# Attention over 8192 context keys: the transposition of a quarter of the softmax integers, and the spreading of the key scales, by other engines

## The chip, the cores and the metric

The kernel runs on one core of one Trainium2 chip. The core has a matrix engine (PE, whose weight loads are listed apart as PEld), a vector engine (DVE), a scalar engine (ACT), a GpSimd engine (POOL) and a sync engine (SP), which mainly issues transfers. ACT and POOL issue transfers too; sixteen DMA engines carry them all. Each engine works through its own instructions in order and waits on semaphores for the others.

The metric is the device time of one execution in microseconds (us), lower is better. Before the change the median of three runs is 2955.57 us (2953.47 to 2957.51).

## The reference, cut to what matters

The program is one block of a perceiver: cross attention of 512 queries on 8192 context tokens, then causal self attention inside each of four sequences, then a feed-forward layer with 4-bit weights. The change touches only the cross attention (and the place of one small load):

```python
q = ((layernorm(x) @ Wq + bq) * scale)        # 512 queries, 16 heads of 64
k, v = split(ctx @ Wkv + bkv)                 # 8192 keys and values
q = _fq_sym(q, axis=-1)                       # integers -127..127 times a scale, per query and head
k = _fq_sym(k, axis=-1)                       # the same, one scale per key and head
v = _fq_sym(v, axis=2)                        # one scale per column of v, over all keys
attn = softmax(einsum('bhqd,bhkd->bhqk', q, k))
attn = _fq_unsigned(attn, axis=-1)            # integers 0..255, scale = row maximum / 255
out = einsum('bhqk,bhkd->bhqd', attn, v) @ Wp + bp
```

So for each head and each query there are 8192 scores. They are products of integers, multiplied by the scale of the key, exponentiated with the row maximum taken off, rounded to integers of 0 to 255, and multiplied with the integers of v. The integers are kept as 16-bit numbers.

## The kernel before

**Stages.** Queries are projected first. Then two passes over the context project the values (V pass) and the keys (K pass), each matrix product in three parts; PE is the engine that is always busy there. In the K pass the keys are quantised on DVE, transposed by a transfer from on-chip memory to on-chip memory (`transpose_k`, L564, a `dma_start_transpose` on SP's queue, 128x512 of 16 bits at a time), copied to a staging tile by ACT (`store_k`, L568) and written to device memory `k_d` by POOL's queue. `key_scales` (L589) does the same for the scales of a quarter of the keys: PE transposes, ACT copies, POOL writes to `sk_d`. The order of the work of these stages is written out by hand: `do(step, function, arguments)` puts an entry on an agenda, and `perform` runs it sorted by step.

**The attention stage** (L711 to L867) then works through 64 units, a unit being one head `h` of 16 and one tile `t` of 128 queries out of 4. A unit has eight groups `g` of 1024 keys. A loop over steps `s`, one group of scores per step, calls the following functions in a fixed order, each with its own lag:

- `scores` (L728), at step `s` for unit `s // 8`: two PE products into PSUM (tile `sc`, two buffers), then one DVE instruction (L748) that multiplies them by the scales of the keys (tile `sk`), writes them as `e`, and keeps the maximum.
- `maximum` (L759), after the eighth group: two small DVE instructions that make the row offset `m`.
- `exponentials` (L771), at groups 0 and 4 of the next unit: one ACT instruction (L776) over 4096 keys, `e` to 16-bit integers `a` (three buffers).
- `transposes` (L785), `LAG_T` = 12 steps behind the scores: four PE transposes of two keys at a time, since they treat pairs of 16-bit integers as one 32-bit word, into PSUM tile `a_pt` (three buffers); then one copy to on-chip memory, tile `aT`. The copy is on DVE for groups 0 and 4 (`COPIES_DVE`), on ACT for the other six.
- `values` (L799), `LAG_V` = 15 steps behind: eight PE products of `aT` with the values `vq`, summed up in PSUM tile `av`. After the last unit of a head four more DVE instructions finish the head (`r`, `xo`).

The tiles that a head needs are loaded during the last query tile of the head before: the keys `kt` (`load_keys`, four of 256 KB) and the scales `sk` (`load_scales`, eight transfers that write 1024 scales to each of 128 partitions, 512 KB each), both on SP's queue. The values of two heads at a time are loaded by `load_values` (L718) as four transfers of 512 KB on POOL's queue, into one of two buffers of 64 groups. Apart from those, SP and POOL have nothing to do in this stage.

**Other lines the change touches.** `shifts` (L369/L370) is a table of 1 KB, loaded on SP's queue ahead of everything else and used in the V pass. L678 is the place of the last `key_scales` in the agenda, at 5 behind the end of the K pass; `store_k` of the last tile stands at 4.

Of the kernel before, what the change touches and what calls it, by code (L numbers as in the profile page):

```python
# [32 lines left out]
F32 = mybir.dt.float32  # L34
BF16 = mybir.dt.bfloat16
# [10 lines left out]
P = 128  # L46
# [15 lines left out]
LAG_V = NSC + 7  # L62
COPIES_DVE = (0, 4)
# [20 lines left out]
def tile_perceiver(  # L84
# [132 lines left out]
    def do(step, fn, *args):  # L217
        agenda.append((step, len(agenda), fn, args))
# [151 lines left out]
    nc.sync.dma_start(out=shifts, in_=nibbles)  # L370
# [77 lines left out]
    do(0.5, load_bq)  # L448
    do(0.5, nc.vector.memset, vmax, 0.0)
# [117 lines left out]

    def store_k(u, n):  # L568
        if u % 2 == 0:
            ksts[n] = pools["k"].tile([P, NP // 2, 256], BF16, name="kst", tag=f"kst{n}", bufs=1)  # L570
        kst = ksts[n]
        nc.scalar.copy(  # L572
            kst.rearrange("p h (n e) -> p h n e", e=2)[:, :, :, u % 2], kTs.pop((u, n))
        )
        if u % 2 == 1:
            c, at_tile = divmod(u, KC // P)
            group, block = divmod(at_tile // 2, SC // 256)
            half, at_block = divmod(block, SC // 512)
            at_key = 512 * group + 256 * at_block
            hs = H // 2 * n  # L580
            for j in range(2):
                nc.gpsimd.dma_start(
                    out=k_d[c][
                        hs + j : hs + H // 2 : 2, half, :, at_key : at_key + 256
                    ].rearrange("p d n -> d p n"),
                    in_=kst[D * j : D * j + D],
                )

    def key_scales(c):  # L589

        row = pools["k"].tile([P, P, 2], F32, name="sk_row", tag="sk_row", bufs=1)
        for e in range(2):
            pt = kv_ps.tile([P, P], F32, name="sk_pt", tag="ps")
            nc.tensor.transpose(pt, sks[c].rearrange("p h (i e) -> p e h i", e=2)[:, e], ident)
            nc.scalar.copy(row[:, :, e], pt)
        nc.gpsimd.dma_start(
            out=sk_d[c].rearrange("h (i n) -> (h i) n", n=2 * P), in_=row.rearrange("p n e -> p (n e)")
        )
# [8 lines left out]
    def load_keys(h, c):  # L607
        kt = pools["keys"].tile([P, KC // 2], BF16, name=f"kt{h}_{c}", tag="kt", bufs=5)
        nc.sync.dma_start(out=kt, in_=k_d[c][h].rearrange("f d n -> (f d) n"))
        kts[h, c] = kt  # L610

    def load_scales(h, g):
        t = pools["keys"].tile([P, SC], F32, name=f"sk{h}_{g}", tag="sk", bufs=9)
        c, half = divmod(g, 2)
        nc.sync.dma_start(out=t, in_=sk_d[c][h, ts(half, SC)].partition_broadcast(P))
        sks_at[h, g] = t
# [45 lines left out]
    for u in range(KT):  # L662
# [14 lines left out]
        if u % (KC // P) == KC // P - 1:  # L677
            do(at + TILE + (5 if u + 1 == KT else 9.5), key_scales, u // (KC // P))  # L678
# [32 lines left out]
    with tc.tile_pool(name="at", bufs=2) as at, tc.tile_pool(  # L711
        name="at_s", bufs=4
    ) as small, tc.tile_pool(name="sc_ps", bufs=2, space=PSUM) as sc_ps, tc.tile_pool(
# [4 lines left out]
        def load_values(p):  # L718
            vq = at.tile([P, KT, P], F16, name=f"vq{p}", tag="vq")
            for c in range(NKC):  # L720
                part = ts(c, KT // NKC)
                nc.gpsimd.dma_start(out=vq[:, part, :], in_=vq_d[p, :, part, :])
            vqs[p] = vq
# [61 lines left out]
        def transposes(n, g):  # L785
# [9 lines left out]
            copy = nc.vector.tensor_copy if g in COPIES_DVE else nc.scalar.copy  # L795
            copy(aT, pt.bitcast(I32))  # L796
            state[n]["aT", g] = aT

        def values(n, g):  # L799
# [4 lines left out]
            aT = state[n].pop(("aT", g)).bitcast(F16).rearrange("p i (q e) -> p i e q", e=2)  # L804
            for i in range(SC // P):
                k = g * (SC // P) + i
                nc.tensor.matmul(  # L807
                    avs[h][:, t, :],
                    lhsT=aT[:, i // 2, i % 2, :],
                    rhs=vqs[p][:, k, ts(j, D)],  # L810
                    start=(k == 0),
                    stop=(k == KT - 1),
                )
            if g < NSC - 1:
                return
# [22 lines left out]
        load_values(0)  # L838
# [8 lines left out]
        with tc.manual_schedule():  # L847
            for s in range(n_steps + LAG_V):
                n, g = divmod(s, NSC)
                if g % (NSC // NEC) == 0 and 1 <= n <= len(units):  # L850
                    exponentials(n - 1, g // (NSC // NEC))
                if n < len(units):
                    h, t = units[n]
                    scores(n, g)
                    if t == NT - 1 and h + 1 < H:
                        if g % 2 == 1:
                            load_keys(h + 1, g // 2)
                        load_scales(h + 1, g)
                    if g == NSC - 1:
                        maximum(n)  # L860
                if at_step(s - LAG_T):
                    transposes(*at_step(s - LAG_T))
                if at_step(s - LAG_V):
                    values(*at_step(s - LAG_V))
                pair, at_pair = divmod(s, 8 * NSC)
                if at_pair == LAG_V and pair + 1 < NP:
                    load_values(pair + 1)  # L867
# [558 lines left out]
```

## Time and profile before

The profiled execution took 2952.94 us, 2.6 us under the median of the three runs; its span, from the first to the last instruction, is 2951.2 us. Of the engines in the whole span and in one unit of the attention stage (10.80 us from one unit's first scores to the next's, away from a change of head):

| engine | busy in the span, us | share | busy in one unit of 10.80 us |
|---|---|---|---|
| PE | 2766.8 | 94% | 8.7 to 9.5 |
| DVE | 2485.6 | 84% | 10.73 |
| ACT | 1342.0 | 45% | 10.58 |
| POOL | 270.5 | 9% | 0 |
| DMA engines, mean | | 44% | 1% to 66% |

The span's rows of tenths cut it into 40 equal slices of 73.8 us. The attention stage lies in slices 20 to 29: its first scores are multiplied on DVE at 1513.24 us, its last at 2218.30 us, and the last product of the values is done at 2233.6 us. An instruction's line can be that of a helper; tile names come without their buffer numbers.

### The profile page before, as it was taken

The numbers are of one execution on the slowest core, as the hardware profiler recorded it, in microseconds if no ns is written. First come the engines' busy times: TensorE is split into PE (matmuls) and PEld (weight loads), VectorE is DVE, ScalarE is ACT, GpSimd is POOL, SyncE is SP. The second block draws the span as 40 slices with busy tenths as digits, with TensorE's granted clock in tenths as the row PEclk, the third lists the DMA queues.
The fourth block names the chain that finished last, engine by engine and source line by source line (L and its number), as shares of the span: only waits on it lengthen the run. The fifth ranks groups of instructions, "written<-read, shape, count | busy, mean of one in ns | idle before, by whom it ended". The sixth has DMA issues, their size and how long they took to land.

```text
span 2951.2 us, 43061 instructions
## 1 busy us (share of the span) xinstructions
PE 2766.8 (94%) x16504; PEld 2166.9 (73%) x16504; DVE 2485.6 (84%) x4074; ACT 1342.0 (45%) x1537; POOL 270.5 (9%) x416
## 2 busy tenths in 40 slices
PE   8999999999999999999978888888888899799998
PEld 3788888888878888888846666666665677688876
DVE  6899998555799998988779999999995898776674
ACT  4212112112323333333249999999995244333332
POOL 0011111000022222222110000000001000000000
PEclk9999999999999999999989999999999999899999
DMA  5555565222457777776354424424413222122222
GB/s 182 176 201 195 192 219 188 93 100 93 145 143 195 189 193 187 196 182 167 90 187 149 161 108 165 172 108 150 159 62 119 68 84 67 50 86 98 95 86 93
DMA packets 203470, 412.76 MB, mean 140 GB/s; under 512 B 91904, under 2 KB 95616, under 8 KB 203264
## 3 DMA queue, kind: packets, MB, share of 16 engines
q1 hardware_dynamic: 158688, 256.37, 27.8%
q0 software_dynamic: 43520, 152.60, 16.2%
q8 instruction: 129, 2.11, 0.3%
q10 hardware_dynamic: 1056, 1.05, 0.2%
q14 instruction: 77, 0.63, 0.1%
HBM read 286.72 MB, written 104.34 MB: 133 GB/s over the span
## 4 chain that ended last, share of the span: by engine, by line
PE 67%; DVE 26%; issue 4%; DMA 2%; ACT 1%; SPq 0%; POOL 0%; DVEq 0%; ACTq 0%
PE kv_a L341 31%; DVE e L748 16%; PE kv_b L341 15%; PE acc_a L984 3%; PE y_a L1329 3%; PE gate_a L162 3%; PE up_a L162 3%; DVE aT L796 2%; PE q_ps L290 2%; PE y_b L1329 1%; PE acc_b L984 1%; PE gate_b L162 1%; PE up_b L162 1%; DVE sw_l L155 1%; PE a_pt L791 1%
## 5 line engine op out<-in xcount | busy, mean ns | idle before, releaser
L341 PE MATMUL kv_b<-w_d,c_d 128*128 128x512 f32 x2048 | 806.0, 394 | 0.8 <-DVE c_d L156 0.8
L341 PE MATMUL kv_a<-w_h,c_h 128*128 128x512 f32 x2048 | 806.4, 394 | 0.0
L341 PE MATMUL kv_a<-w_l,c_l 128*128 128x512 f32 x2048 | 806.1, 394 | 0.2 <-ACT w_l L244 0.2
L748 DVE CUSTOM_DVE_ANT_0 e<-sc,sk 128x1024 f32<-128x1024 f32 x512 | 600.7, 1218 | 9.9 <-DMA k_d<-kst 8.6
L776 ACT ACTIVATE a<-e,m,sq 128x4096 int16<-128x4096 f32 x128 | 487.6, 3809 | 29.7 <-DVE m L765 29.7
L341 PEld LDWEIGHTS kv_a<-w_l,c_l 128*128 128x128 f32 x2048 | 384.8, 188 | 89.8 <-ACT w_l L244 0.6
L341 PEld LDWEIGHTS kv_b<-w_d,c_d 128*128 128x128 f32 x2048 | 384.8, 188 | 89.8 <-DVE c_d L156 1.1
L341 PEld LDWEIGHTS kv_a<-w_h,c_h 128*128 128x128 f32 x2048 | 384.9, 188 | 88.9 <-issue 0.2
L791 PE MATMUL a_pt<-ident,a 128*128 128x128 f32 x2048 | 338.4, 288 | 6.8 <-ACT aT L796 3.7
L152 ACT ACTIVATE c_h<-c_raw 128x1024 fp32r<-128x1024 f32 x128 | 135.0, 1055 | 420.1 <-PE kv_a L341 413.0
L355 DVE SCALAR_TENSOR_TENSOR f<-kv_a,bkv 128x512 f32<-128x512 f32 x256 | 175.9, 687 | 163.9 <-PE kv_a L341 163.2
L791 PEld LDWEIGHTS a_pt<-ident,a 128*128 128x128 f32 x2048 | 216.4, 142 | 127.1 <-issue 64.5
L741 PE MATMUL sc<-kt,qT 64*128 64x512 bf16 x1024 | 203.4, 390 | 97.1 <-DVE mx L748 93.2
L572 ACT CAST kst<-kT 128x512 bf16<-128x512 int16 x128 | 99.4, 777 | 309.3 <-DMA kT<-ki 309.2
L807 PE MATMUL av<-vq,aT 128*128 128x64 f16 x4096 | 203.3, 193 | 11.4 <-DVE xo L822 11.4
L807 PEld LDWEIGHTS <-aT 128*128 128x128 f16 x4096 | 189.8, 98 | 19.9 <-issue 14.0
L796 ACT COPY aT<-a_pt 128x512 int32<-128x512 int32 x384 | 198.8, 593 | 1.3 <-PE a_pt L791 1.1
L356 DVE SCALAR_TENSOR_TENSOR f<-kv_b,f 128x512 f32<-128x512 f32 x256 | 176.7, 690 | 20.0 <-DVE f L355 1.4
L155 DVE TENSOR_TENSOR fw_l<-fw_raw,fw_h 128x1024 fp32r<-128x1024 f32 x64 | 78.3, 1224 | 107.1 <-ACT fw_h L152 106.9
L155 DVE TENSOR_TENSOR c_l<-c_raw,c_h 128x1024 fp32r<-128x1024 f32 x128 | 155.8, 1217 | 6.6 <-ACT c_h L152 6.2
L741 PEld LDWEIGHTS <-qT 64*128 64x128 bf16 x1024 | 67.3, 93 | 125.7 <-issue 96.2
L156 DVE SCALAR_TENSOR_TENSOR c_d<-c_l,c_raw 128x1024 fp32r<-128x1024 f32 x128 | 156.3, 1221 | 2.3
(186 smaller groups left out, 3763.5 us busy)
## 6 DMA issues: line engine op xcount, KB each, us to landing
c_raw<-in_ctxT SPq DMA_DIRECT2D x128, 512.0 KB, 3.6
sk<-sk_d SPq DMA_DIRECT2D x128, 512.0 KB, 6.7
v_d<-f POOLq DMA_DIRECT2D x64, 512.0 KB, 3.1
vl<-v_d POOLq DMA_DIRECT2D x64, 512.0 KB, 4.2
gu_d<-w_ffn POOLq DMA_DIRECT2D x44, 512.0 KB, 3.1
fw_raw<-gu_d SPq DMA_DIRECT2D x42, 512.0 KB, 3.3
k_d<-kst POOLq DMA_DIRECT2D x128, 128.0 KB, 3.6
vq_d<-vq POOLq DMA_DIRECT2D x32, 512.0 KB, 5.2
```

The costliest lines, as they stand in the source:

```text
L155: nc.vector.tensor_tensor(lo, src, hi, ALU.subtract)
L156: nc.vector.scalar_tensor_tensor(df, lo, -1.0 - UP, src, ALU.mult, ALU.add)
L162: nc.tensor.matmul(ps, lhsT=lhs(i, k), rhs=rhs(i, k), start=(k == 0 and i != 1), stop=(k == NC - 1 and i != 0),)
L341: nc.tensor.matmul(ps, lhsT=tokens[s][i][:, k, :], rhs=w3[s < KT][k][i][:, ts(n, 512)], start=(k == 0 and i != 1), stop=(k == NC - 1 and i ...
L355: nc.vector.scalar_tensor_tensor(f, a, 1.0 + 1.0 / UP, bias[s < KT][n], ALU.mult, ALU.add)
L356: nc.vector.scalar_tensor_tensor(f, b, -1.0 / UP, f, ALU.mult, ALU.add)
L741: nc.tensor.matmul(ps[:, ts(i, 512)], lhsT=qT[rows, h, ts(t, P)], rhs=kts[h, g // 2][rows, ts(g % 2, 512)], start=True, stop=True,)
L748: nc.vector.tensor_tensor_reduce(out=state[n]["e"][-1][:, ts(g % (NSC // NEC), SC)], in0=ps, in1=sks_at[h, g], scale=1.0, scalar=LOWEST, o ...
L776: nc.scalar.activation(a, st["e"][c], AF.Exp, bias=st["m"], scale=sq[:, t, h : h + 1], accum_out=sums[h][:, t, c : c + 1],)
L791: nc.tensor.transpose(pt[:, i, :], a[:, at_word + P * i : at_word + P * i + P], ident)
L796: copy(aT, pt.bitcast(I32))
L807: nc.tensor.matmul(avs[h][:, t, :], lhsT=aT[:, i // 2, i % 2, :], rhs=vqs[p][:, k, ts(j, D)], start=(k == 0), stop=(k == KT - 1),)
```

## The change

It does five things.

1. **A quarter of the keys (`DMA_KC` = 1, groups 2 and 3 of each unit) is no longer transposed by PE.** `dma_transposes` issues one transposing transfer per unit on SP's queue, 128x2048 integers of `a` into a tile `aT_d` (two buffers). It is called at step 4 of the next unit; the products of these two groups come 20 steps behind their scores (`LAG_D`), those of the other groups 16 instead of 15.
2. **Only group 4 is copied by DVE** (`COPY_DVE`); groups 0, 1, 5, 6 and 7 by ACT.
3. **The scales of a head are spread by POOL.** `load_rows` brings the scales of a head as four rows of 8 KB to partitions 0, 32, 64 and 96; `spread_scales` is a GpSimd `partition_broadcast` of 1024 of them to 128 partitions, eight for a head, in place of the eight transfers of 512 KB. The first head's scales still come by transfer. The scales get 8 buffers instead of 9, the keys 6 instead of 5, and the keys are asked for at groups 0 to 3 instead of 1, 3, 5 and 7.
4. **The values come in quarters** with five buffers of 16 groups (`order` puts the quarter of the transferred keys last), each asked for as soon as its buffer is read out.
5. **Small moves:** `shifts` is loaded at agenda step 32; the last `key_scales` goes from 5 to 3.9, ahead of `store_k` of the last tile; the keys of the transferred quarter are stored in plain order instead of even and odd ones interleaved (`in_order`), since the transfer keeps single integers apart and PE's transposition pairs; the small pool `at_s` is opened ahead of `at`.

```diff
-LAG_V = NSC + 7
-COPIES_DVE = (0, 4)
+LAG_V = NSC + 8
+COPY_DVE = 4
+DMA_KC = 1
+LAG_D = NSC + 12
...
-    nc.sync.dma_start(out=shifts, in_=nibbles)
...
+    do(32, lambda: nc.sync.dma_start(out=shifts, in_=nibbles))
...
+    def in_order(t, c):
+        dims = "p h" if len(t.shape) == 3 else "p"
+        if c == DMA_KC:
+            return t.rearrange(f"{dims} (e n) -> {dims} n e", e=2)
+        return t.rearrange(f"{dims} (n e) -> {dims} n e", e=2)
...
-        nc.scalar.copy(
-            kst.rearrange("p h (n e) -> p h n e", e=2)[:, :, :, u % 2], kTs.pop((u, n))
-        )
+        nc.scalar.copy(in_order(kst, c)[:, :, :, u % 2], kTs.pop((u, n)))
...
-        kt = pools["keys"].tile([P, KC // 2], BF16, name=f"kt{h}_{c}", tag="kt", bufs=5)
+        kt = pools["keys"].tile([P, KC // 2], BF16, name=f"kt{h}_{c}", tag="kt", bufs=6)
...
+    def tile_of_scales(h, g):
+        sks_at[h, g] = pools["keys"].tile([P, SC], F32, name=f"sk{h}_{g}", tag="sk", bufs=NSC)
+        return sks_at[h, g]
...
-            do(at + TILE + (5 if u + 1 == KT else 9.5), key_scales, u // (KC // P))
+            do(at + TILE + (3.9 if u + 1 == KT else 9.5), key_scales, u // (KC // P))
...
-        def load_values(p):
-            vq = at.tile([P, KT, P], F16, name=f"vq{p}", tag="vq")
+        def load_values(p, c):
+            vqs[p, c] = at.tile([P, KT // NKC, P], F16, name=f"vq{p}_{c}", tag="vq", bufs=NKC + 1)
+            nc.gpsimd.dma_start(out=vqs[p, c], in_=vq_d[p, :, ts(c, KT // NKC), :])
+
+        def load_rows(h):
+            sks_at[h] = at.tile([P, KC], F32, name=f"sk_row{h}", tag="sk_row", bufs=1)
             for c in range(NKC):
-                part = ts(c, KT // NKC)
-                nc.gpsimd.dma_start(out=vq[:, part, :], in_=vq_d[p, :, part, :])
-            vqs[p] = vq
+                nc.gpsimd.dma_start(out=sks_at[h][32 * c : 32 * c + 1, :], in_=sk_d[c][h : h + 1, :])
+
+        def spread_scales(h, g):
+            c, half = divmod(g, 2)
+            nc.gpsimd.partition_broadcast(
+                tile_of_scales(h, g), sks_at[h][32 * c : 32 * c + 1, ts(half, SC)], channels=P
+            )
...
-            copy = nc.vector.tensor_copy if g in COPIES_DVE else nc.scalar.copy
+            copy = nc.vector.tensor_copy if g == COPY_DVE else nc.scalar.copy
...
+        def dma_transposes(n):
+            at_key = DMA_KC * KC % EC
+            a = state[n]["a"][DMA_KC * KC // EC][:, at_key : at_key + KC].bitcast(F16)
+            aT = at.tile([P, KC // P, P], F16, name="aT_d", tag="aT_d")
+            nc.sync.dma_start_transpose(out=aT, in_=a)
...
-        load_values(0)
+        order = [c for c in range(NKC) if c != DMA_KC] + [DMA_KC]
+        load_rows(1)
...
-            for s in range(n_steps + LAG_V):
+            for s in range(n_steps + LAG_D):
                 n, g = divmod(s, NSC)
+                if s == 1:
+                    for c in order:
+                        load_values(0, c)
+                if g == NSC // NEC and 1 <= n <= len(units):
+                    dma_transposes(n - 1)
                 if g % (NSC // NEC) == 0 and 1 <= n <= len(units):
                     exponentials(n - 1, g // (NSC // NEC))
...
                     if t == NT - 1 and h + 1 < H:
-                        if g % 2 == 1:
-                            load_keys(h + 1, g // 2)
-                        load_scales(h + 1, g)
+                        if g < NKC:
+                            load_keys(h + 1, g)
+                        spread_scales(h + 1, g)
+                        if g == NSC - 1 and h + 2 < H:
+                            load_rows(h + 2)
...
-                if at_step(s - LAG_T):
-                    transposes(*at_step(s - LAG_T))
-                if at_step(s - LAG_V):
-                    values(*at_step(s - LAG_V))
-                pair, at_pair = divmod(s, 8 * NSC)
-                if at_pair == LAG_V and pair + 1 < NP:
-                    load_values(pair + 1)
+                for lag, work, dma in (
+                    (LAG_T, transposes, False),
+                    (LAG_V, values, False),
+                    (LAG_D, values, True),
+                ):
+                    at_lag = at_step(s - lag)
+                    if at_lag and (at_lag[1] * SC // KC == DMA_KC) == dma:
+                        work(*at_lag)
+
+                pair, since = divmod(s - NSC * (2 * NT - 1), NSC * 2 * NT)
+                if 0 <= pair < NP - 1 and since in (0, LAG_V + 1, LAG_V + 5, LAG_V + 7):
+                    load_values(pair + 1, order[(0, LAG_V + 1, LAG_V + 5, LAG_V + 7).index(since)])
```

## The prediction

> **What bounds the kernel now.** I read the share of busy time first, then the waits of the attention stage, then one unit of it in order of time. The page's rows of tenths show where each engine is full:
>
> ```profile
> PE   8999999999999999999978888888888899799998
> ...
> DVE  6899998555799998988779999999995898776674
> ACT  4212112112323333333249999999995244333332
> ```
>
> PE is full outside the attention stage; inside it (slices 20 to 29) DVE and ACT both are. Which of the two ends last? The waits between 1520 and 2220 us (who waited, for whom: total, times, longest):
>
> ```profile
> PE sc L741 <- DVE mx L748: 84.6, 191, 1.0
> ...
> ACT a L776 <- DVE m L765: 29.5, 62, 1.3
> ```
>
> PE and ACT wait for DVE, ACT once in each unit, and no wait of DVE's is anywhere near: between 1700 and 1900 us DVE's multiply L748 has 0.0 us of idle time before it. So DVE sets the pace. Its instructions in one unit (start, duration, us):
>
> ```profile
> 1600.46 1.23 DVE L748 CUSTOM_DVE_ANT_0 e<-sc,sk 128x1024 f32<-128x1024 f32 x1
> ...
> 1601.61 0.69 DVE L796 COPY aT<-a_pt 128x512 int32<-128x512 int32 x1
> 1602.21 1.22 DVE L748 CUSTOM_DVE_ANT_0 e<-sc,sk 128x1024 f32<-128x1024 f32 x1
> ...
> 1603.35 1.22 DVE L748 CUSTOM_DVE_ANT_0 e<-sc,sk 128x1024 f32<-128x1024 f32 x1
> ...
> 1611.13 0.21 DVE L765 TENSOR_SCALAR m<-m,nsq 128x1 f32<-128x1 f32 x1
> 1611.26 1.22 DVE L748 CUSTOM_DVE_ANT_0 e<-sc,sk 128x1024 f32<-128x1024 f32 x1
> ```
>
> Instructions overlap by some 0.08 us, so count from start to start: a multiply takes 1.145 (1602.21 to 1603.35), a copy behind it adds 1602.21 - 1600.46 - 1.145 = 0.605, and from the last multiply's end to the next unit's first 0.44 go to `m`. A unit is 8 x 1.145 + 2 x 0.605 + 0.44 = 10.81; measured 10.80.
>
> **Part 1, one copy less on DVE.** A unit becomes 9.16 + 0.605 + 0.44 = 10.20. The copy of group 0 of each unit runs inside the next one, so it leaves DVE's path 63 times (the 64th is in the drain): 63 x 0.605 = **-38.1 us**, if nothing else is late.
>
> *ACT, next in line.* From the same timeline: an exponential starts at 1600.56, its three copies at 1604.36, the next exponential at 1605.79, so 3.80 and 0.48 per copy in sequence: 10.46 per unit with six. With five it is 9.98, under 10.20 by 0.2. That thin margin is what is late next.
>
> *PE* does eight of its 32 transposes less. A step holds scores 0.32, transposes 0.49, values 0.33 (starts at 1604.63, 1604.98, 1605.47, 1605.80): 1.14 at most before. With the new lags, steps 0, 1, 4, 5 hold all three, steps 2, 3 no values, steps 6, 7 two groups of values (0.98). It stays under DVE's 1.145 everywhere and gains slack. The PSUM buffers: six groups rotate over three, each copied by ACT or DVE before its turn, as now.
>
> **Part 2, the transposing transfer.** The nearest row is the K pass's transfer of a quarter of the size (SP's issue min/median/max ns, and time to landing):
>
> ```profile
> L566 SPq DMA_TRANSPOSE kT<-ki x128: 1189/1191/2864, 808.5 to 1504.7; - x128
> ...
> DMA to landing us min/median/max: 2.4/3.1/9.2
> ```
>
> Issue: four times 1.19 = 4.8 us of SP's queue, if it goes with size. Bytes: the first of them, alone on the engines, shows as
>
> ```profile
> 809.50:810.00 0.50, 0.50 (x4) 0.41 (x3) 0.50 (x1) 0.00 (x0) 0.00 (x0) 1.00 0.55 111
> 810.00:810.50 0.50, 0.50 (x3) 0.39 (x3) 0.50 (x2) 0.00 (x0) 0.09 (x1) 1.00 0.76 152
> ```
>
> (last two columns: DMA share, GB/s): 0.5 x 111 + 0.5 x 152 = 131 KB for 0.655 us of all sixteen engines, 200 GB/s. So 512 KB need 2.6 us. [...] Landing is then about 4.8 + 1.7 = 6.5 us after the start (from the median 3.1 - 1.19 = 1.9 behind the issue); bounds: 3.1 (issue doesn't grow) and 4 x 3.1 = 12.4. The exponential ends 3.9 us into a unit, and PE wants the result at step 6 of the unit after, about 16.5: a cover of 12.6 us. The second cover is shorter: tile `a` has three buffers, and ACT's second exponential of the next unit overwrites it at 15.4, 11.5 us after the start. At 6.5 us both hold; at 12.4 ACT would lose 0.9 per unit. Cost taken: 0. On SP's queue behind it are only the keys of the next head, and it is behind theirs for one unit in four: the fourth key load waits for group 3's scores, at about 5.2 instead of 3.9, and 1.3 of 11.5 us is spent.
>
> DMA load falls: eight broadcasts of 512 KB per head go, four transposing transfers of 512 KB come.
>
> **Part 3, spreading by GpSimd.** A spread may start when the multiply of the same group has read the buffer, and must be done for that group a unit later. If a spread takes T, the eighth ends 1.15 + 8T into the head's last unit, and is wanted at 10.20 + 7 x 1.145 + 0.605 = 18.8: **T up to 2.2 us costs nothing**. No spread is in the trace. Its bounds by POOL's own rows (us, mean ns):
>
> ```profile
> L522 POOL PARTITION_ALL_REDUCE vall<-vmax x1 | 3.2, 3247 | 12.8 <-DVE ki L187 12.8
> ...
> masks.py:199 POOL TENSOR_SCALAR_AFFINE_SELECT ident<-ident 128x128 f32<-128x128 f32 x1 | 0.3, 293 | 0.3 <-POOL ident masks.py:197 0.3
> ...
> masks.py:197 POOL MEMSET ident<- 128x128 f32 x1 | 0.2, 204 | 0.3 <-POOLq L1416 0.3
> ```
>
> A memset of one column takes 101 ns, so writing costs (204 - 101) / 128 = 0.8 ns an element: 0.9 us for 1024, the low end. The all-reduce on 128x1024 reduces over partitions and then spreads: 3.25, the high end. Reading one operand and writing it, the select, comes to (293 - 101) / 128 = 1.5 ns, **1.6 us**; it is the nearest and I take it. [...] By 1.6 the eighth is done at 13.9, 4.9 us early; by 2.2 the sum is the same, with no cover left.
>
> Does a busy POOL slow DVE? The later adds on POOL show both cases:
>
> ```profile
> 2343.17 5.82 POOL L934 TENSOR_TENSOR x<-x,row 128x512 f32<-128x512 f32 x4 [87.84 <-DMA row<-in_abo]
> 2343.56 0.69 DVE L996 SCALAR_TENSOR_TENSOR f<-acc_b,f 128x512 f32<-128x512 f32 x1
> ...
> 2346.22 1.65 DVE L1052 TENSOR_TENSOR f<-f,cs 128x512 f32<-128x512 f32 x1
> ```
>
> With both operands in on-chip memory (L1052) DVE takes 1.65 instead of its median 0.69; with one operand in PSUM (L996) it takes its usual 0.69. The multiply reads `sc` from PSUM, the copy reads PSUM alone: cost 0. Only the `xo` product might meet a spread.
>
> POOL's queue: the row loads and value quarters are issues of 0.53 us each. A quarter is asked for when PE has read the buffer and is needed 7 steps (8.9 us) later at the tightest; four loads at once landed in 6.0 at the median. Nothing waits. Keys: six buffers, asked for earlier; nothing.
>
> **Part 4, the ends.** `shifts` off SP's queue lets the first load of x start at 0.73 instead of 1.18: -0.4 (ends 0 and -0.5), the chain starts with it; at its new place SP is idle. With `key_scales` ahead, its store no longer stands between the last casts and the last key stores on POOL (0.56 us): the stage starts 0.4 earlier, as the first multiply waits for those stores. Pipeline fill: the values come later by the four row loads (2.1 us), to about 1521, wanted at 1533. Drain: after the last exponential ACT does five copies instead of six: -0.5; the last transposing transfer lands before. The plain order of stored keys changes only an access pattern of ACT, which idles there.
>
> **Sum:** 38.1 + 0.4 + 0.4 + 0.5 = 39.4. Profiled: 2952.9 - 39.4 = 2913.5; the median of the runs lies 2.6 above the profiled one, so **2916 us**.
>
> **Rivals.**
> - *The spread is the bound (slower).* At T = 3.25 the eighth spread ends at 27.1, DVE stalls 8.3 us at each of 15 changes of head: +125, about 3041. The gain is eaten where 15 x (8T - 17.7) = 39, at T = 2.55. For it: the all-reduce, and POOL's rows are rough. Against: a spread does only part of that work. With any loss from POOL blocking DVE: 11%.
> - *Another cover is too thin (part of the gain).* If ACT's 0.2 margin or the transfers' 11.5 us fail, a unit takes about 10.5: 64 x 0.3 = 19 us gained, 2936. For it: ACT is 10.58 of 10.80 busy; one K transfer landed only after 9.2. Against: that one stood in a queue of scale broadcasts that no longer exists. 9%.
> - *PE is the hidden bound (no change).* Its step of 1.14 equals DVE's 1.145, so the freed 0.6 would turn into a wait for scores: 2956. Against: PE waits for DVE 191 times, DVE hardly for PE. 2%.
>
> The forecast has 78%, itself 2908 to 2924. Below it lie only small things at the ends. To leave no more than two in ten out, the range takes in the second rival: 2907 to 2938. Differences under 0.2% (6 us) can't be told from none here: faster 0.86, same 0.02, slower 0.12.
>
> **What would show it.** Right: DVE's unit at 10.20 with one copy; ACT still waiting a little for `m`; a spread under 2.2 us; multiplies at 1.22 beside it; the transfer landing within 11 us. Wrong: multiplies waiting for POOL at each fourth unit (spread too slow), exponentials waiting for a DMA, or values waiting for `aT_d`.

## The result, and the profile after

The changed kernel takes 2917.65 us in the median of four runs (2917.13 to 2925.09); the kernel before, on the same chip, 2956.1 (2953.47 to 2957.51). The ratio is 0.9877, 95% interval 0.9859 to 0.9894. The profiled execution took 2917.71 us, its span 2915.9: 35.3 less than before, where the sum of the prediction said 39.4. By the medians it is 38.4 less; the runs of one kernel spread over 4 us before and 8 after.

The rows of tenths of the changed kernel:

```profile
PE   8999999999999999999978888888878899799998
...
DVE  6899998555799888989769999999995898676674
ACT  4212121111323333333229999999994244333332
POOL 0011111000022222222113223322311000000000
```

DVE and ACT are still both full in the attention stage, which is shorter; POOL, empty there before, is two to three tenths busy. The waits between 1520 and 2200 us (who waited for whom: total, times, longest):

```profile
POOL sk L741 <- DVE mx L768: 332.3, 23, 29.7
...
PE sc L761 <- DVE mx L768: 87.7, 265, 1.0
...
ACT a L796 <- DVE m L785: 14.2, 16, 1.5
```

The others still wait for DVE. POOL waits for it too, 332 us: its spreads are early. ACT's waits for `m` have gone from 62 to 16, so ACT has almost caught up. One unit on DVE:

```profile
1606.87 0.21 DVE L785 TENSOR_SCALAR m<-m,nsq 128x1 f32<-128x1 f32 x1
1606.99 1.22 DVE L768 CUSTOM_DVE_ANT_0 e<-sc,sk 128x1024 f32<-128x1024 f32 x1
...
1608.13 0.69 DVE L816 COPY aT<-a_pt 128x512 int32<-128x512 int32 x1
1608.74 1.22 DVE L768 CUSTOM_DVE_ANT_0 e<-sc,sk 128x1024 f32<-128x1024 f32 x1
...
1617.06 0.21 DVE L785 TENSOR_SCALAR m<-m,nsq 128x1 f32<-128x1 f32 x1
```

From `m` to `m` it is 10.19 us, with one copy in it, and no gap. The two operations that no trace had shown:

```profile
L741 POOL PARTITION_BROADCAST sk<-sk_row x120 | 143.2, 1297 | 332.7 <-DVE mx L768 332.3
```

```profile
L825 SPq DMA_TRANSPOSE aT_d<-a x64: 1665/1983/3858, 1528.5 to 2186.7; - x64
...
DMA to landing us min/median/max: 4.2/4.4/6.9
```

The first row is from the costliest groups: a spread takes 1.30 us. The second view is that of the tile `aT_d`: SP issues the transfer in 1.98 us (median), and it lands after 4.4.

Where the time went, from starts in the two traces, us:

| stretch | before | after | difference | forecast |
|---|---|---|---|---|
| start to the first product of the context | 77.57 | 76.04 | -1.5 | -0.4 |
| from there to the last quantisation of keys | 1426.37 | 1425.26 | -1.1 | 0 |
| from there to the first multiply of the attention stage | 9.30 | 12.12 | +2.8 | -0.4 |
| first to last multiply | 705.06 | 667.67 | -37.4 | -38.1 |
| last multiply to the last `xo` | 15.77 | 15.31 | -0.5 | -0.5 |
| from there to the end | 717.10 | 719.54 | +2.4 | 0 |

### The profile page after: what moved, and what is told of

Same layout as the page of the kernel before. It is cut to its first block, busy times and chain, and to the rows that moved or that the text cites. A ratio compares the mean times of both kernels' runs of the same rounds, so it can differ in the third digit from the quotient of the medians.

```text
span 2915.9 us, 42024 instructions
## 1 busy us (share of the span) xinstructions
PE 2714.9 (93%) x15992; PEld 2103.4 (72%) x15992; DVE 2447.8 (84%) x4010; ACT 1308.2 (45%) x1473; POOL 442.0 (15%) x596
## 2 busy tenths in 40 slices
DMA packets 321226, 383.83 MB, mean 132 GB/s; under 512 B 224064, under 2 KB 228736, under 8 KB 321024
## 3 DMA queue, kind: packets, MB, share of 16 engines
q10 hardware_dynamic: 1056, 1.05, 0.2%
## 4 chain that ended last, share of the span: by engine, by line
PE 69%; DVE 16%; issue 8%; ACT 5%; DMA 1%; POOL 0%; SPq 0%; DVEq 0%; ACTq 0%; POOLq 0%
PE kv_a L344 32%; PE kv_b L344 16%; DVE e L768 10%; PE y_a L1376 3%; PE gate_a L165 3%; PE up_a L165 3%; PE acc_a L1031 3%; ACT aT L816 2%; ACT a L796 2%; PE q_ps L293 2%; PE y_b L1376 1%; PE gate_b L165 1%; PE up_b L165 1%; PE acc_b L1031 1%; PE a_pt L811 1%
## 5 line engine op out<-in xcount | busy, mean ns | idle before, releaser
L768 DVE CUSTOM_DVE_ANT_0 e<-sc,sk 128x1024 f32<-128x1024 f32 x512 | 595.1, 1218 | 13.1 <-DMA kt<-k_d 11.4
L811 PE MATMUL a_pt<-ident,a 128*128 128x128 f32 x1536 | 253.9, 288 | 13.0 <-ACT a L796 7.9
L811 PEld LDWEIGHTS a_pt<-ident,a 128*128 128x128 f32 x1536 | 162.6, 142 | 104.2 <-issue 49.7
L741 POOL PARTITION_BROADCAST sk<-sk_row x120 | 143.2, 1297 | 332.7 <-DVE mx L768 332.3
L761 PEld LDWEIGHTS <-qT 64*128 64x128 bf16 x1024 | 76.6, 93 | 148.8 <-issue 106.7
L816 ACT COPY aT<-a_pt 128x512 int32<-128x512 int32 x320 | 168.4, 586 | 3.8 <-PE a_pt L811 3.6
L839 PE MATMUL av<-vq,aT 128*128 128x64 f16 x3072 | 154.3, 194 | 14.4 <-DVE xo L854 14.4
L839 PEld LDWEIGHTS <-aT 128*128 128x128 f16 x3072 | 130.2, 99 | 49.0 <-issue 43.8
```

What stands on the lines that cost most here:

```text
L741: nc.gpsimd.partition_broadcast(tile_of_scales(h, g), sks_at[h][32 * c : 32 * c + 1, ts(half, SC)], channels=P)
L761: nc.tensor.matmul(ps[:, ts(i, 512)], lhsT=qT[rows, h, ts(t, P)], rhs=kts[h, g // 2][rows, ts(g % 2, 512)], start=True, stop=True,)
L768: nc.vector.tensor_tensor_reduce(out=state[n]["e"][-1][:, ts(g % (NSC // NEC), SC)], in0=ps, in1=sks_at[h, g], scale=1.0, scalar=LOWEST, o ...
L811: nc.tensor.transpose(pt[:, i, :], a[:, at_word + P * i : at_word + P * i + P], ident)
L839: nc.tensor.matmul(avs[h][:, t, :], lhsT=aT, rhs=vqs[p, c][:, k, ts(j, D)], start=(g == 0 and i == 0), stop=(last and i == SC // P - 1),)
```

## The experiments

Unless it says otherwise, edits are made to the changed kernel. All times are medians, and a ratio is to the kernel before, run in the same series, where it took 2952.7 to 2957.4. Times of different series can differ by that much, so across series the ratios count.

**1. Both copies on DVE.** Everything of the change stays but the copy that leaves DVE.

```diff
-            copy = nc.vector.tensor_copy if g == COPY_DVE else nc.scalar.copy
+            copy = nc.vector.tensor_copy if g in (0, COPY_DVE) else nc.scalar.copy
```

> The changed kernel with DVE copying group 0 again (as before the change), everything else new: the transposing transfer, the spreads, the quarters. Theory: DVE's instructions alone set the unit, so it goes back to 8 x 1.145 + 2 x 0.605 + 0.44 = 10.80 us and the time to 2917.7 + 38 = 2956 us. Rival: the gain comes from the eight PE transposes or the 60 MB of broadcasts that are gone; then the time stays near 2918 (at most 2925), and DVE shows idle time before its multiplies.

Measured: 2955.54 us, ratio 1.0002 (0.9993 to 1.0011), units (after the first two) of 10.79 to 10.82, those at a change of head 11.84 to 11.98. The transfer, the spreads and the quarters are worth nothing by themselves, and cost nothing: the one copy is the whole gain. Their part is to make room for it.

**2. Every spread done twice.**

```diff
+            t = tile_of_scales(h, g)
+            for _ in range(2):
-            nc.gpsimd.partition_broadcast(
-                tile_of_scales(h, g), sks_at[h][32 * c : 32 * c + 1, ts(half, SC)], channels=P
-            )
+                nc.gpsimd.partition_broadcast(
+                    t, sks_at[h][32 * c : 32 * c + 1, ts(half, SC)], channels=P
+                )
```

> Each spread of key scales is done twice in a row, to double its price; the output is the same. The trace of the changed kernel has 1.30 us for one spread, so T = 2.6. Theory of the deadline: the eighth ends 1.15 + 8 x 2.6 = 21.9 us into the last unit of a head and is wanted at 18.8, so DVE stalls 3.1 us at each of 15 changes of head: +47 us, 2964 us, with the wait named at the multiplies. Rival: POOL has more cover than that (or less[...]): below +20 us, or above +80 us with multiplies longer than 1.22 us.

Measured: 2975.07 us, ratio 1.0067 (1.0052 to 1.0082), 57.4 over the changed kernel where 47 was expected. The waits of this kernel (1520 to 2220 us), and then POOL in order of time at one change of head:

```profile
DVE e L770 <- POOL sk L743: 44.3, 37, 1.3
```

```profile
1591.85 2.68 POOL L743 PARTITION_BROADCAST sk<-sk_row  x2 [22.84 <-DVE mx L770]
1594.37 0.57 POOL L731 DMA_DIRECT2D vq<-vq_d  x1
1594.95 11.47 POOL L743 PARTITION_BROADCAST sk<-sk_row  x9
```

Now DVE waits for POOL. The unit into a new head is 10.22 + 3.03 = 13.25 us, or 13.80 in every second head, where the issue of a value load (0.57) stands between the spreads. The stall by the prediction's rule is 8 x 2.60 - 17.7 = 3.1. So the rule and its cover of 17.7 us hold for the stall itself. The value issue, which I had left out, is 4 of the 10 us of excess. Another 5 lie in the units right behind a stall: PE idles in the stall, and its granted clock is 0.50 right after it, 13 times between 1540 and 2150 us against once in the changed kernel. The multiplies keep 1.22 us beside a POOL that works without a pause: no contention.

**3. All scales by transfers, none by POOL.**

```diff
-        load_rows(1)
...
-                        spread_scales(h + 1, g)
-                        if g == NSC - 1 and h + 2 < H:
-                            load_rows(h + 2)
+                        load_scales(h + 1, g)
```

> The changed kernel with the scales of every head loaded by SP's broadcasting transfers of 512 KB, as before the change; no row loads and no spreads. Theory: the spread isn't what gains, but it keeps SP's queue free for the transposing transfer. In the last unit of a head 4 MB of scales, 1 MB of keys and the transfer stand in one queue, some 13 us at 400 GB/s for a unit of 10.2: the transfer starts only after the scales of group 4 (about 7 us in) and lands after 15, so some 2 to 5 us are lost per head, 30 to 75 us in all: 2950 to 2990. Rival: transfers have room enough; within 6 us of 2918.

Measured: 2970.55 us, ratio 1.0052 (1.0037 to 1.0067). Waits (1520 to 2220 us), then the tile `sk`:

```profile
DVE e L768 <- DMA sk<-sk_d: 49.7, 22, 4.3
...
ACT a L796 <- DMA aT_d<-a: 4.5, 6, 1.5
```

```profile
L624 SPq DMA_DIRECT2D sk<-sk_d x120: 319/371/1579, 1542.4 to 2195.2; - x120
...
DMA to landing us min/median/max: 3.6/6.3/9.3
```

The scales are late at the changes of head: units there take up to 15 us. SP's queue in the unit before such a change shows why:

```profile
1592.24 7.66 SPq L825 DMA_TRANSPOSE aT_d<-a  x1
1599.99 1.96 SPq L624 DMA_DIRECT2D sk<-sk_d  x4
```

The time lies in the range that was expected, but not for the expected reason. It is not the transfer that comes late for lack of room (exponentials wait 4.5 us for it), it is the scales behind it: issued behind the loads, a transposing transfer holds SP for 6.5 to 7.8 us at each of the 15 changes of head, and the scales of group 4 go out 5.9 to 7.2 us after their buffer is free. DVE's waits at group 4 make 44 us. Since the buffer was free so long, the one scales buffer less (8 instead of 9) isn't the cause. So the spreads are needed, though not for their own speed: they take the scales out of the queue in which the transfer stands, and 4 MB a head off the DMA engines, which are busy all the time there (a share of 1.03 from 1590 to 1600 us). The 400 GB/s of the expectation lie in what the kernel before moves at such shares: 354 to 416 GB/s at 1.00 to 1.04, in stretches of 3.41 us between 1553 and 1605 us.

**4. Half of the keys by transfers, no copy on DVE.** Groups 2, 3, 6 and 7; all values then come 20 steps behind the scores.

```diff
-LAG_V = NSC + 8
-COPY_DVE = 4
-DMA_KC = 1
+LAG_V = NSC + 12
+COPY_DVE = -1
+DMA_KCS = (1, 3)
...
+                if g == 0 and 2 <= n <= len(units) + 1:
+                    dma_transposes(n - 2, 3)
                 if g == NSC // NEC and 1 <= n <= len(units):
-                    dma_transposes(n - 1)
+                    dma_transposes(n - 1, 1)
```

> Two quarters of the softmax integers (groups 2, 3, 6, 7) by transposing transfers, the other four groups' copies all on ACT, none on DVE; all values 20 steps behind. If DVE's instructions set the unit: 8 x 1.145 + 0.44 = 9.60 us, ACT needs 2 x 3.80 + 4 x 0.48 = 9.52, SP's queue 2 x 2.0 of issue: 63 x 0.6 = 38 us less than the changed kernel, 2880 us. Rival: two transfers of 512 KB a unit (5.2 us of all DMA engines at 200 GB/s, beside keys and values) land too late, or ACT's margin of 0.08 is too thin: 2890 to 2920 with exponentials or values waiting.

Measured: 2888.17 us, ratio 0.9771 (0.9756 to 0.9785). The unit is 9.60 in most places, as worked out, and the time beats both kernels. But 8 us of the expected gain is missing: eight units are 0.6 to 1.1 us too long, and DVE waits there for scores. Around one of them (per engine busy us, then granted PE clock, DMA share, GB/s):

```profile
core 0: us, PE busy (x) PEld busy (x) DVE busy (x) ACT busy (x) POOL busy (x), PEclk, DMA share, GB/s
1613.49:1616.90 3.41, 2.08 (x24) 1.32 (x24) 3.38 (x9) 3.41 (x5) 0.37 (x1) 1.00 1.26 226
1616.90:1620.31 3.41, 3.22 (x27) 2.11 (x27) 2.89 (x7) 3.41 (x1) 0.00 (x0) 0.50 1.19 262
1620.31:1623.73 3.42, 3.15 (x46) 2.31 (x44) 3.35 (x7) 1.80 (x5) 0.00 (x0) 1.00 0.77 57
```

For 3.41 us PE is granted half its clock and falls behind. There are eight such stretches in the stage, and the eight long units lie at them. In the 3.41 us ahead of each, PE was busy only 0.55 to 0.63 of the time (here 2.08 of 3.41). Experiments 9 and 10 test that.

**5. No copy on DVE, one quarter by transfer.** `COPY_DVE = -1`: ACT copies all six groups.

> The changed kernel with the last DVE copy (group 4) given to ACT too: DVE copies nothing, ACT copies six groups per unit; one quarter still goes by transfer. Theory (the prediction's ACT need of 3.80 per exponential and 0.48 per copy in sequence): DVE alone would need 9.16 + 0.44 = 9.60 per unit, but ACT needs 2 x 3.80 + 6 x 0.48 = 10.48, more than the 10.20 it had to keep up with, so ACT becomes the bound: the unit is 10.4 to 10.5, 64 x 0.25 = 16 us over the changed kernel, about 2934 (2928 to 2940), and the waits show ACT's exponentials waiting no more for m while DVE waits for PE's scores, and those for ACT's copies. Rival (ACT has more room than its sequence shows, or the transfers set the pace): unit 9.60, 2917.7 - 63 x 0.605 = about 2880.

Measured: 2985.66 us, ratio 1.0105 (1.0089 to 1.0122): slower than the kernel before, and 52 us over what was expected. Plain units take 10.70, many others 11.8 to 13.2. PE in order of time, then the windows around:

```profile
1637.21 0.39 PE L761 MATMUL sc<-kt,qT 64*128 64x512 bf16 x2 [0.17 <-DVE mx L768]
1639.33 0.66 PE L811 MATMUL a_pt<-ident,a 128*128 128x128 f32 x4 [1.73 <-ACT aT L816]
1639.92 0.39 PE L761 MATMUL sc<-kt,qT 64*128 64x512 bf16 x2
1640.24 1.12 PE L811 MATMUL a_pt<-ident,a 128*128 128x128 f32 x4
```

```profile
1636.79:1640.20 3.41, 1.52 (x11) 0.72 (x9) 2.66 (x6) 3.41 (x5) 3.41 (x4) 1.00 0.42 111
1640.20:1643.61 3.41, 3.41 (x28) 2.72 (x26) 2.46 (x4) 3.30 (x3) 1.98 (x2) 0.50 0.78 148
```

Two things happen. With nothing copied during an exponential, the transposes of group 7 stand 1.73 us in PE's queue until ACT has emptied a PSUM buffer, and the next scores stand behind them. DVE gets those late, `m` comes late, and ACT, whose own work would fill 10.46, waits for `m`. And PE, busy for only 1.52 of 3.41 us, has half its clock for the next 3.41 us: four transposes take 1.12 us instead of 0.66. Experiment 10 separates the two.

**6. Every transposing transfer twice.**

```diff
-            nc.sync.dma_start_transpose(out=aT, in_=a)
+            for _ in range(2):
+                nc.sync.dma_start_transpose(out=aT, in_=a)
```

> The changed kernel with each transposing transfer issued twice in a row into the same tile, so that twice the issue time and twice the bytes lie between the exponential and PE's values. Theory (the transfers have a wide cover): the second one lands about 2 x 1.98 + 2.5 = 6.5 us after the first is issued, near 9 where keys are loaded beside it, under the 11.5 us at which ACT wants buffer a back: no change, within 6 us of 2918, no ACT wait for aT_d or a, unit 10.20. Rival (the cover is nearly used up, the prediction's second rival): ACT's exponentials wait for the transfer and values for aT_d, the unit is 10.4 or more, 2930 or more.

Measured: 2929.06 us (2921.0 to 2937.37), ratio 0.9912 (0.9888 to 0.9935), 11.4 us more than the changed kernel. Neither side is met in full: units are 10.20 in most places, but 13 exponentials wait for the transfer, 12.8 us in all. SP and ACT in order of time at one of them:

```profile
1587.14 4.14 SPq L615 DMA_DIRECT2D kt<-k_d  x4
1591.57 12.78 SPq L826 DMA_TRANSPOSE aT_d<-a  x3
```

```profile
1604.45 3.80 ACT L796 ACTIVATE a<-e,m,sq 128x4096 int16<-128x4096 f32 x1 [1.27 <-DMA aT_d<-a]
```

Most of the waits come in pairs, once in two heads: the first behind the key loads, which share the queue as here, the second two units later, while the values of the next two heads come in. Five of the six half-clock stretches of this stage follow such waits. The experiment was also harder than I meant it to be: in all 64 pairs the second transfer is issued only when the first has landed, since both write the same tile. A pair lands 9.3 us after its first issue in the median and 13.5 at most, not 6.5, and the cover is 11.5. So the cover holds twice the time of the transfer in most units, and not where keys or values are loaded beside it.

**7. Both moves at the ends undone.** `shifts` first on SP's queue, the last `key_scales` at 5.

> The changed kernel with the two small moves at the ends undone: shifts is loaded ahead of everything on SP's queue again, and the last key_scales is back at 5, behind store_k of the last tile. By the prediction each was worth 0.4: 2918.5, not told from 2917.7 by the time, but by the trace: the first context product should start 0.4 later (76.0 to 76.4; 77.5 if shifts made the whole difference of the two traces), and the attention stage's first multiply 0.4 later behind the last key quantisation (12.5 instead of 12.1). Rival (the earlier key_scales is what made the stage start later in the changed kernel): that distance falls back to 9.3, and the time by about 2 us.

Measured: 2918.19 us (2915.75 to 2922.59). The first context product starts at 77.66, 1.6 later than in the changed kernel; in the twelve traces with `shifts` late it starts at 75.1 to 76.8, in the two with it first at 77.6 and 77.7. The first multiply comes 9.70 behind the last quantisation, not 12.12. So the late `shifts` gains about 1.6 us, and the early `key_scales` loses 2.4: together nothing that the time shows.

**8. The order of the pools undone.**

> The changed kernel with the pool of small tiles opened behind the other again, as before the change: only where tiles lie in on-chip memory differs, and so which earlier tile a new one has to wait for. If the order of the pools set the late start of the attention stage (12.1 us from the last key quantisation to the first multiply, 9.3 before the change) or the late first weight load behind it, the distance goes back to about 9.3, or the 719.5 us behind the stage to about 717: 2 to 5 us less, 2913 to 2916. Rival (the order of transfers on the queues sets both): nothing moves, 2917.7 within 2 us.

Measured: 2916.43 us (2915.67 to 2917.57), distance 11.68, 718.1 us behind the stage: the rival's side; the order of the pools sets neither.

**9. More work for PE: half of the keys by transfers, scores of four groups done twice.**

```diff
-            for i in range(2):
+            for i in list(range(2)) * (2 if g % 4 > 1 else 1):
```

> The kernel of two quarters by transfer with more work for PE and none less: in groups 2, 3, 6 and 7, whose steps have no transposes, the two products of the scores are done twice into the same PSUM tile (the same output). In e4_two_quarters eight stretches of 3.4 us between 1575 and 2110 us have a granted PE clock of 0.50, each behind a stretch in which PE was busy 0.57 to 0.65 of the time, and the eight long units (7.7 us over the others in all) lie at them. Theory (the clock is taken back because PE is too idle, and that makes DVE wait for scores): with 1.28 us more per unit of 9.60 the clock stays at 1.00, the waits of DVE for sc vanish, every unit is 9.60 or 10.65, and the time falls by about 7, to 2881. Rival (the long units come from transfers or buffers, and PE's time counts): the repeated scores come on top, the time stays at 2888 or grows by up to 64 x 1.28 = 82.

Measured: 2885.11 us (2878.84 to 2887.73), ratio 0.9753 (0.9738 to 0.9767), 3 less than without the repetition; the intervals of the two ratios overlap, so the time alone doesn't tell a small gain from none. In the stage of the traces the theory is met: no half-clock stretch is left between 1540 and 2150 us, DVE's waits for scores fall from 7.4 us to 1.3, from `m` to `m` all but one of the units after the first are 9.59 to 9.62, or 10.65 to 10.67 at a change of head (one is 9.72), and the stage is 631.4 us long instead of 638.5. Half of it is given back outside: the first multiply stands 12.52 behind the last quantisation, 8.69 without the repetition.

**10. More work for PE: no copy on DVE, scores of group 3 done four times.**

```diff
-            for i in range(2):
+            for i in list(range(2)) * (4 if g == 3 else 1):
```

> The kernel without any DVE copy, e5_no_dve_copy, with the scores of group 3 done four times into the same PSUM tile (the same output), 0.97 us more of PE time in each unit at the place where PE then waits 1.7 us for ACT's copies. In e5 24 stretches of 3.4 us between 1540 and 2240 us have a granted PE clock of 0.50, each behind one in which PE was busy 0.45 to 0.56 of the time. Theory (two causes in e5: PE's queue stands behind ACT's copies, which makes a unit 10.70, and the clock, which adds about 1.4 at each such stretch): the half-clock stretches go, the units become 10.70 and 11.8 throughout, and the time falls by about 24 x 1.4 = 33 us, to about 2952. Rival (the long units of e5 come from the copies alone and the low clock only accompanies them): no gain, 2985 or more.

Measured: 2933.77 us (2932.23 to 2937.93), ratio 0.9926 (0.9914 to 0.9939), 52 less than experiment 5 with work added and none removed. Two windows of the stage of this kernel, and then its wait of DVE for scores (1520 to 2220 us):

```profile
1700.00:1900.00 200.00, 171.72 (x2064) 114.57 (x2064) 185.26 (x357) 197.62 (x191) 60.23 (x66) 1.00 0.47 106
1900.00:2100.00 200.00, 171.65 (x2042) 114.18 (x2040) 185.33 (x355) 197.71 (x187) 53.18 (x61) 1.00 0.43 94
```

```profile
DVE e L768 <- PE sc L761: 44.1, 52, 0.9
```

The clock is 1.00 where experiment 5 had 0.91 and 0.89, from `m` to `m` all units after the first two are 10.69 to 10.74, and ACT is busy 197.6 of 200 us; what DVE's waits for scores do is told below, at ACT's margin. More stretches went than the 24 I had counted: over the whole stage experiment 5 has 119 us at half clock, 35 stretches, which is 60 us of PE's time at 1.71 each. (Read over whole stretches, the shares of busy time ahead of them are 0.41 to 0.56 in experiment 5 and 0.55 to 0.63 in experiment 4, a little lower than the two expectations say.) This settles experiment 5: with the half-clock stretches gone and everything else kept, ACT's copies cost 2933.8 - 2917.7 = 16 us. The other 52 go with the clock; in the two traces 44 of them lie in the stage.

**11. Experiment 9 with the last `key_scales` back at 5.**

> The kernel of e9_two_quarters_busy with the last key_scales back at 5, behind store_k of the last tile, as before the change; shifts stays late. In e9 the first multiply stands 12.5 us behind the last key quantisation, in e4_two_quarters 8.7, in e7_ends_before, where key_scales is at 5, 9.7. Theory (the earlier key_scales lets the scales' load go out ahead of the last keys' load, which then lands late): the distance is 9.3 to 9.9, 2.7 us less than in e9, about 2882. Rival (the distance varies from one build or execution to another, whatever the order): it stays near 12, 2885.

Measured: 2882.02 us (2876.52 to 2882.56), ratio 0.9755 (0.974 to 0.9769); distance 9.44. The median is the lowest of all; the ratio of 0.9755 against the changed kernel's 0.9877 is some 36 us. Against experiment 9 there is no difference by the ratio (0.9755 and 0.9753), though the first multiply comes 3.1 us earlier in the trace.

**12. The changed kernel with `key_scales` back at 5 alone.**

> The changed kernel with only the last key_scales back at 5; shifts stays late. Theory (the earlier key_scales costs the start of the stage 2.4 us, shifts gains about 2 at the start of the kernel): last key quantisation at about 1501.5, first multiply 9.3 to 9.9 later instead of 12.1, so 2915.3. Rival (the distance varies for another reason): near 12, 2917.7.

Measured: 2918.21 us (2915.49 to 2919.92). SP and the first multiply of DVE in order of time, first in the changed kernel, then here:

```profile
1507.80 0.32 SPq L624 DMA_DIRECT2D sk<-sk_d  x1
1508.78 0.32 SPq L615 DMA_DIRECT2D kt<-k_d  x1
...
1513.42 1.22 DVE L768 CUSTOM_DVE_ANT_0 e<-sc,sk 128x1024 f32<-128x1024 f32 x1 [11.43 <-DMA kt<-k_d]
```

```profile
1508.28 0.32 SPq L615 DMA_DIRECT2D kt<-k_d  x1
1508.92 0.79 SPq L624 DMA_DIRECT2D sk<-sk_d  x2
...
1510.60 1.22 DVE L768 CUSTOM_DVE_ANT_0 e<-sc,sk 128x1024 f32<-128x1024 f32 x1 [8.24 <-DMA k_d<-kst]
```

With `key_scales` early, the load of the scales goes out ahead of the last keys' load, and the first multiply starts 2.8 us later. The wait is put down to those keys, but it isn't theirs: in experiments 5 and 8 the multiply starts 1.1 and 1.4 us before they land. In all fourteen traces it starts 0.65 or 0.66 us after the last store of keys (`k_d`, 128 KB, on POOL's queue) has landed. For that one store, first in the changed kernel, then here:

```profile
DMA to landing us min/median/max: 5.1/5.1/5.1
```

```profile
DMA to landing us min/median/max: 3.2/3.2/3.2
```

Where the first load of scales goes out within 1.1 us of the last store, as in the changed kernel (0.2), the store lands after 4.5 to 5.7 us (eight traces); where it goes out 1.6 us or more behind, after 3.0 to 3.4 (six). That the two share the DMA engines is the likely reason, but it is argued and not shown. The time doesn't show the 2.8 us: from the last multiply on, this execution took 5.0 us longer. That part of the program is the same in all these kernels, and from the last `xo` to the end it took 716.5 to 722.9 us in the traces.

## Why the prediction held, by its own steps

*The bound and the unit (-38.1).* Right: DVE's unit is 10.19 to 10.23, forecast 10.20, and the stage is 37.4 shorter. About half of the missing 0.7 is in the second unit, while the pipeline fills: it is 0.3 shorter, not 0.6. Experiment 1 puts the whole gain on that copy, experiment 4 takes the second one off with the same 0.6 per unit.

*ACT's margin.* Right that it is thin and comes next. What I had not seen is the way in which it fails. With six copies the unit is 10.70 and not 10.46, since ACT, PE and DVE wait for each other in a ring, and 10.46 is only ACT's work: in experiment 10 an exponential starts at 1803.49, right behind `m`, which ends at 1803.45, where ACT by its own sequence would have started it at 1803.23. The head change's extra 1.05 us on DVE vanishes in the same waits. That experiment 10 still comes out 16 us over the changed kernel, as six copies at 0.48 had given, is luck: the expectation had ACT's unit some 0.25 too short, and left out the 0.26 per unit (a quarter of the head change) that DVE needed before; the two cancel.

*PE.* "It gains slack" was right and half the story. With too much of it (PE busy 0.63 or less of a stretch of 3.41 us in experiments 4 and 5) the granted clock fell from 1.00 to 0.50 in the next, which no step of the prediction looked at. The changed kernel sits near that: its lowest stretches of 3.41 us are busy 0.61 to 0.62, those of the kernel before 0.64. Both kernels enter the stage at half clock, until 1532 us; after that one half-clock stretch lies between the multiplies of the changed kernel (at 2037 us), which its DVE units don't show, and none in the kernel before.

*The transposing transfer (cost 0).* The cost is right, both terms were too large. The issue was put at 4.8 us, four times the smaller one; it is 1.98. The landing was put at 6.5; it is 4.4, 6.9 at most. "If it goes with size" is the term that failed: four times the bytes cost 1.7 times the issue. Of the 11.5 us of cover 4.6 remain at the slowest; experiment 6 uses them up. The issue of 1.98 holds only for a queue that is not crowded: behind the loads of experiment 3 it is 6.5 to 7.8.

*The spread (T = 1.6 us, free to 2.2).* Right side, 1.30 measured; the select with one operand (293 ns for 128x128) was the nearest row. A row with two operands would have misled: POOL's add of two 128x512 tiles (`x` and `sv_bp`, L934) has a median of 1.27 us in the kernel before, by size an estimate of 2.5 us for 1024 elements, nearly twice what the spread takes. The eighth spread is done 18.8 - 1.15 - 8 x 1.30 = 7.3 us before it is wanted. The rival's rule 15 x (8T - 17.7) stood the test of experiment 2: it gives 47 at T = 2.60, measured 57. The stalls themselves are 46 by the trace; the rest is 4 of value issues and what follows a stall, which the rule doesn't hold.

*No contention.* Right: multiplies take 1.218 us on average in both kernels.

*The ends (-1.3 in all).* Here most of the missing 4 us of the two traces lie. The late `shifts` was put at -0.4 and gave about 1.6; why it gives more than its own 0.45 wasn't followed up. The early `key_scales` was put at -0.4 and costs 2.4 to 2.8. That the first multiply waits for the key stores was right: it starts 0.65 us behind the last of them in every trace. But the step counted only the stores on POOL, and not the load that the early store sets free on SP, 512 KB of scales, beside which the last key store needs 5.1 us instead of 3.2. Experiments 3 and 4 have the same order and yet start 8.8 and 8.7 us behind the last quantisation: there the stores go out earlier, the last one 1.6 us ahead of that load, and it lands after 3.0. Why they go out earlier there is open. The 2.4 us at the end of the program, and the 1.1 us between the first context product and the last quantisation (1425.3 to 1426.2 in the traces of the same code), are not clear of what the same code varies by. So that the median lies within 2 us of the forecast is in part luck.

*Rivals.* The first is excluded by T, the third by the unit. The second, a cover that is too thin, was not met, but experiments 5 and 6 show how near it was: one copy more on ACT, or one transfer more on the queue. The copy more cost not a part of the gain, as that rival had it, but all of it, most of it through the clock.

## What to carry to other kernels

If two engines are nearly full, count what each would need after the move, but also look at what stands in PE's queue behind a wait: a few tenths of margin on ACT became a ring of waits (a unit of 10.70 us instead of 10.46). Taking work from a PE that isn't the bound cost it half its clock in places (0.50 in experiments 4 and 5); read the granted clock next to the busy share before and after, and if it is halved in places, giving PE work that isn't needed is a cheap test of the cause and may even stay in. An issue that is moved earlier also lets out what waits for it on another queue (here 512 KB of scales, beside which a store landed after 5.1 us instead of 3.2): follow that one too. And when a wait is put down to a transfer, compare the landings with the start of the waiter in several traces before believing the name.

## What the hardware showed that was not expected

- **The clock was halved without an idle stretch.** Between 1540 and 2150 us of all fourteen traces the granted clock goes from full to half (1.00 to 0.50) 71 times. In the 3.41 us ahead of each change PE was busy between 0.14 and 0.63 of the time; no stretch busier than 0.63 was followed by one, and some at 0.51 to 0.63 were not either: a partly idle stretch was enough, though not always. Half clock lasted one such stretch or two (in the changed kernel one, from 2037.36 to 2040.77 us). The work added for PE lifts the lowest stretch from 0.55 to 0.65 (experiment 9) and from 0.41 to 0.59 (experiment 10), and no change is left there. All changes behind 1490 us fall on one raster of 3.413 us within a trace, to 0.01 us, and its place differs from trace to trace. The busy time of PE is modelled at its ends, so 0.63 is a mark for these traces.
- **The issue of a transposing transfer grew little with its size.** 1.19 us for 128x512 and 1.98 for 128x2048 of 16 bits, in the median. What stood in the queue ahead of it counted more: 6.5 to 7.8 us behind four loads of scales and three of keys (experiment 3).
- **Fewer bytes, more packets.** HBM reads fall from 286.7 to 224.3 MB, while packets go from 203470 to 321226, those under 512 bytes from 91904 to 224064: the 64 transposing transfers move 131072 packets of 256 bytes, 2048 each. No wait in the trace of the changed kernel is put down to one of them.
